# A whole network on one core: where group norms, keys, scores and experts get their turns and their PSUM places

## The chip, the cores and the metric

The kernel runs on one core of one Trainium2 chip. A core has five engines that this text names as the profile does: PE (matrix products; PEld is its loading of weights), DVE (vector), ACT (functions), POOL (GpSimd) and SP, which here only issues DMAs. Each runs its own list of instructions in order; they meet through semaphores. The metric is the device time of the one core, in microseconds, median of several runs: 15310.87 us before the change (15308.61 to 15326.58, three runs).

## The reference

The input x is 4 x 32 x 96 x 256, that is 4 batches of 3072 tokens with 256 channels, float32 throughout. Two layers are computed:

```python
x = x + mamba_d(mamba_t(group_norm(x)))          # two state space scans, along 96 and along 32
t = tokens(x)
t = t + attention(layer_norm(t))                 # additive attention, no matrix product of q and k:
#   h = tanh(q[:, :, None, :] + k[:, None, :, :] + bh);  e = h @ Wa;  softmax(e) @ inputs
t = t + experts(layer_norm(t), edges)            # gates from a graph, then 4 experts, 2 of them kept
#   per node: softmax over its incoming edges (1048576 random ones and one to itself), layer norm,
#   top 2 of 4 scores -> gate;  out = sum over e of gate[e] * (gelu(x @ W1[e] + b1[e]) @ W2[e] + b2[e])
```

group_norm has 32 groups of 8 channels, so each batch needs a mean and a variance of all its 3072 tokens before its first block can start. The additive attention needs a tanh for each triple of query, key and one of 32 units: 4 x 3072 x 3072 x 32 values, which are 3072 ACT instructions of 128 x 3072 here. An edge's gate input is a gathered table row, fetched by POOL with one indirect DMA for 128 edges.

## The kernel before

**Layer 0** (class Layer0, run) works in 64 blocks of 384 tokens: 8 of way t and 8 of way d for each of the 4 batches, with the first t block of the next batch drawn ahead. A block has 48 slots. The states of a block are scanned by DVE (L402) with decays from ACT (L385), inputs and outputs broadcast by DMA (bB, bC) and products on POOL (L409). While block n is scanned, front() prepares block n+1 in the same slots. The first 17 blocks ("lead") run alone, with more of the work on PE and ACT. group_norm (L99 to L132) stands before all of them: for each of 4 batches and 2 halves of the channels it loads the tokens in two halves (xs, two buffers), takes bn_stats on DVE, averages over the groups with two tiny matmuls, and takes the root on ACT.

**Attention** (units, L776 to L865) yields between its steps, and the main loop gives two steps of `steps()` to each iteration of units: half a slot of layer 0 each, as long as there is one, then sort and experts. An iteration issues one th (tanh, L815), scores two iterations later (L788, 16 PE records), and after 8 of them the unit's tail: maximum nb on DVE, exponential pr on ACT, transposes ptw, values pv. side is a list of small generators (keys of the next batch, the layer norm after attention); `beside()` advances the first by one step. keys(b) has 48 steps for a batch: 12 for statistics, then 12 groups of three (normalize, transpose through PE, project with PE and copy to krep and qsel). While a batch has no keys, an iteration issues no th:

```python
yield
late, self.later = self.later, []
for f in late:
    f()
yield
beside()
continue
```

The scores of a unit lie in `pe`, one place of two PSUM banks (pool "ate"). The first scores of a unit overwrite what pr of the unit before reads, so they are held back behind the iteration's second step (`held`).

**After layer 0** steps() gives an iteration to: the sort of the edges on DVE (class Edges, at EDGE_US of estimated work an iteration), the counting products on PE (L1233) and early experts (`early`, L1644 on), which draw on one budget of PE time: SLOT_US an iteration, less what the unit's own steps cost. Early experts put a first product into ph (pool "fp", two banks), copy it out with the bias on DVE (h), and their results (ko) go to DRAM (`kept`). Experts.bank chooses a pool by a turn that ph and po share.

**The tail** (tail, L1730 on) is a table of due times t. Three values of t are one expert unit (512 rows by one expert). Part m of 36 (12 columns of edges: scores, three times spread on DVE and place on PE) falls on t = G0 + PART * m // 2. `some` issues RATE gathers on POOL at each of its five calls a unit, each after a `pace` instruction that reads what ACT or DVE just wrote, so that POOL doesn't run ahead. When a quarter's parts are done, gates follow, and the kept results are loaded, gated and added.

Of the kernel before, what the change touches and what calls it, by code (L numbers as in the profile page):

```python
# [62 lines left out]
FIRST, RATE = 14, 2.75  # L63
G0, PART = 10, 6
KO_BUFS = 2
SLOT_US, PRODUCT_US = 1.2, 0.11
# [8 lines left out]
class Layer0:  # L75
# [8 lines left out]
    def __init__(self, ctx, tc, ident, a, x1):  # L84
# [12 lines left out]
        self.group_norm()  # L97

    def group_norm(self):  # L99

        nc, wk, ps, const = self.nc, self.wk, self.ps, self.const
        gavg = const.tile([P, P], F32, tag="gavg", name="gavg")
        nc.sync.dma_start(gavg, self.a["gavg"])
        eps = const.tile([P, 1], F32, tag="eps", name="eps")
        nc.vector.memset(eps, 1e-5)
        self.gm = const.tile([P, KC, B], F32, tag="gm", name="gm")
        self.gr = const.tile([P, KC, B], F32, tag="gr", name="gr")
        HB = TOK // 2
        NB = HB // 512
        for b in range(B):  # L110
            gm = self.gm[:, :, b]
            mv = wk.tile([P, KC, 2], F32, tag="gmv", name="gmv")
            gv = wk.tile([P, KC], F32, tag="gv", name="gv")
            for k in range(KC):
                stats = wk.tile([P, 2, NB, 6], F32, tag="gst", name="gst")
                for i in range(2):
                    xs = wk.tile([P, HB], F32, tag="dt", name="xs", bufs=2)
                    nc.sync.dma_start(xs, self.a["xT"][k * P:(k + 1) * P, b, i * HB:(i + 1) * HB])
                    for j in range(NB):
                        nc.vector.bn_stats(stats[:, i, j, :], xs[:, j * 512:(j + 1) * 512])  # L120
                nc.vector.bn_aggr(mv[:, k, :], stats.rearrange("p i n s -> p (i n s)"))
            pg = ps.tile([P, T], F32, tag="pp", name="pg")
            nc.tensor.matmul(pg[:, :KC], gavg, mv[:, :, 0], start=True, stop=True)
            nc.vector.tensor_copy(gm, pg[:, :KC])
# [4 lines left out]
            pg2 = ps.tile([P, T], F32, tag="pp", name="pg2")  # L129
            nc.tensor.matmul(pg2[:, :KC], gavg, gv, start=True, stop=True)  # L130
            nc.scalar.activation(self.gr[:, :, b], pg2[:, :KC], AF.Sqrt, bias=eps)
        nc.vector.reciprocal(self.gr, self.gr)  # L132
# [419 lines left out]
    def run(self):  # L552
# [34 lines left out]
        for n, blk in enumerate(blocks):  # L587
# [15 lines left out]
            ahead = self.front(then, blk["lead"]) if then and not breaks else {}  # L603
            for slot in range(48):
# [3 lines left out]
                for part in (left[1], jobs[1], ending, ahead):  # L608
# [31 lines left out]
class Attention:  # L640
# [4 lines left out]
    def __init__(self, ctx, tc, ident, a, x1, x2, xn2T, tab_s, tab_a):  # L645
# [7 lines left out]
        self.ps_e = pool("ate", PE_BUFS, space=PSUM)  # L653
# [122 lines left out]
    def units(self, side):  # L776
# [24 lines left out]
        while i < B * PER + LAG or todo or self.later:  # L801
            b, col = self.entry, self.col = divmod(i, PER)
            if b < B and "krep" not in self.state[b]:
# [3 lines left out]
                for f in late:  # L807
                    f()
                yield
# [15 lines left out]
            if behind and i >= LAG:  # L825
                n, k = divmod(i - LAG, NK)
                if k == 0:

                    pe = self.ps_e.tile([P, 2, JB], F32, tag="pe", name="pe")
# [743 lines left out]
class Experts:  # L1573
# [3 lines left out]
    def __init__(self, ctx, tc, x2, xn2T, gates, out, dram, beside=None):  # L1577
# [363 lines left out]
def whole(tc, a, dram, out):  # L1941
# [11 lines left out]
    with ExitStack() as ctx:  # L1953
        actx, lctx, ectx = ExitStack(), ExitStack(), ExitStack()
        with tc.manual_schedule(engines={E.PE, E.Activation, E.DVE, E.Pool}):
# [10 lines left out]
            def steps():  # L1966
# [7 lines left out]
                lctx.close()  # L1974
                keep = ctx.enter_context(tc.tile_pool(name="late", bufs=1))
# [134 lines left out]
```

## Time and profile before

The profiled execution took 15328.57 us (its span is 15326.8), 17.7 us above the median of the runs. Stages, from the busy time by stretch and the first and last th:

| stretch (us) | what runs | length |
|---|---|---|
| 0 to 62 | group norms of all batches | 62 |
| 62 to 2367 | first block's front, 17 lead blocks of 125 to 135 | 2305 |
| 2367 to 2566 | keys of batch 0, no th | 199 |
| 2566 to 11417 | th beside layer 0; from 5489 to 5574 no th (keys of batch 1) | 8851 |
| 11417 to 12450 | th beside the sort; 268 th | 1033 |
| 12450 to 14205 | th beside counts and early experts; 580 th | 1755 |
| 14205 to 15327 | rest of early experts, tail | 1122 |

Of the page, engines over the whole span, and slices in tenths:

```profile
PE 11744.9 (77%) x86496; PEld 5137.0 (34%) x86496; DVE 11006.6 (72%) x15895; ACT 12153.9 (79%) x9327; POOL 8997.6 (59%) x6935
...
DVE  7888888777777887777777877577778864321367
ACT  3443334999999979999999899999997889999221
POOL 4555556777777767767767677477750024400684
```

Shares over the whole span say little here, since each stage has another leader; the rows of slices show it: DVE in the first seven, ACT after, and no single one at the end. In a group's line "busy, mean ns | idle before" the last part names what ended the idle time of that engine before these instructions.

### The profile page before, as it was taken

To read this page: it belongs to the slowest core of one execution; us is meant where nothing else is said; L and a number is where in the kernel's file an instruction comes from. 1 tells how busy PE (TensorE), PEld (TensorE's weight loads), DVE (VectorE), ACT (ScalarE), POOL (GpSimd) and SP (SyncE) were. 2 spreads that over 40 slices of the span, in tenths; PEclk is the share of its full clock that TensorE was granted. 3 is DMA by queue.
4 is the path that set the end of the run, shared out by engine and by line. 5 is a ranking of instruction groups with operands and counts; after the bars stand their busy time and mean duration, and the time that the engine had idled before them with its cause. 6 is when DMAs were issued, how large, how long until landed. Compare 5 with 4: busy or idle time off the path is not lost. (4 is left out here: it accounts for less than half of the span.)

```text
span 15326.8 us, 225317 instructions
## 1 busy us (share of the span) xinstructions
PE 11744.9 (77%) x86496; PEld 5137.0 (34%) x86496; DVE 11006.6 (72%) x15895; ACT 12153.9 (79%) x9327; POOL 8997.6 (59%) x6935
## 2 busy tenths in 40 slices
PE   5666764777777767788887777888876778988997
PEld 2222332222222233333333333333332334433554
DVE  7888888777777887777777877577778864321367
ACT  3443334999999979999999899999997889999221
POOL 4555556777777767767767677477750024400684
PEclk8888887888888888989998889999988989999998
DMA  5666665445445444454454444355531000010234
GB/s 192 204 203 200 198 204 167 149 148 156 152 150 151 158 156 148 150 152 151 151 150 156 147 149 152 110 156 151 154 127 37 24 13 13 10 31 22 66 95 138
DMA packets 1209121, 2007.93 MB, mean 131 GB/s; under 512 B 412384, under 2 KB 655712, under 8 KB 1204960
## 3 DMA queue, kind: packets, MB, share of 16 engines
q1 hardware_dynamic: 1180384, 1988.07, 41.6%
q0 software_dynamic: 27648, 5.36, 0.8%
q8 instruction: 680, 11.14, 0.3%
q14 instruction: 409, 3.35, 0.1%
HBM read 1875.19 MB, written 117.83 MB: 130 GB/s over the span
## 5 line engine op out<-in xcount | busy, mean ns | idle before, releaser
L815 ACT ACTIVATE th<-krep,qsel 128x3072 f32<-128x3072 f32 x3072 | 8661.7, 2848 | 411.1 <-PE pe L788 392.0
L788 PE MATMUL pe<-th,wa_blk 128*32 128x384 f32 x49152 | 4999.3, 535 | 1196.7 <-ACT pr L884 957.3
L409 POOL TENSOR_TENSOR h<-h,bC 128x768 f32<-128x768 f32 x2048 | 3756.2, 1834 | 3000.4 <-DVE h L402 2634.4
L402 DVE TENSOR_TENSOR_SCAN h<-dA,dB 128x384 f32<-128x384 f32 x4096 | 3687.3, 942 | 1109.4 <-ACT dA L385 752.9
L788 PEld LDWEIGHTS pe<-th,wa_blk 128*32 128x32 f32 x49152 | 1448.0, 116 | 3775.6 <-issue 1992.1
L393 DVE TENSOR_TENSOR dB<-bB,dtu 128x768 f32<-128x768 f32 x2048 | 1942.3, 948 | 123.3 <-DMA bB<-bc 91.2
L385 ACT ACTIVATE dA<-dt,t_A 128x380 f32<-128x380 f32 x2048 | 1127.1, 571 | 887.6 <-DVE h L402 883.1
L385 ACT ACTIVATE dA<-dt,d_A 128x372 f32<-128x372 f32 x2048 | 1102.9, 562 | 601.3 <-DVE h L402 595.9
L428 PE MATMUL py<-h,ident 128*128 128x384 f32 x2176 | 1010.1, 597 | 679.6 <-POOL h L409 678.2
L416 POOL TENSOR_TENSOR h<-h 128x768 f32<-128x768 f32 x752 | 1423.0, 1892 | 53.6
L900 PE MATMUL pv<-xn,pT 128*32 128x257 f32 x18432 | 1116.1, 391 | 172.3 <-DVE pT L893 171.4
L959 POOL TENSOR_SCALAR sf<-sel,f 128x32 f32<-128x32 f32 x384 | 148.6, 410 | 1641.6 <-ACT f L955 1533.9
L893 DVE COPY pT<-ptw 128x512 f32<-128x512 f32 (+1 forms) x768 | 419.0, 546 | 703.7 <-PE ptw L891 703.0
L428 PEld LDWEIGHTS py<-h,ident 128*128 128x128 f32 x2176 | 445.4, 223 | 1247.6 <-POOL h L409 1015.2
L900 PEld LDWEIGHTS pv<-xn,pT 128*32 128x32 f32 x18432 | 583.5, 112 | 759.7 <-DVE pT L893 317.4
L417 POOL TENSOR_TENSOR h<-h 128x384 f32<-128x384 f32 x752 | 783.7, 1042 | 59.0
L418 POOL TENSOR_TENSOR y<-y,h 128x384 f32<-128x384 f32 x752 | 779.9, 1037 | 59.0
L1714 ACT ACTIVATE h<-ph,b 128x512 f32<-128x512 f32 x148 | 96.7, 685 | 662.9 <-POOL pace L1047 473.9
L1337 POOL DMA_INDIRECT gs<-tab_s,si x432 | 526.6, 1219 | 131.3 <-issue 98.8
L891 PE MATMUL ptw<-ident,pr 128*128 128x128 f32 x2304 | 484.7, 328 | 143.5 <-DVE pT L893 79.6
L902 DVE COPY pvs<-pv 128x257 f32<-128x257 f32 x384 | 160.2, 417 | 569.0 <-PE pv L900 568.8
L1052 POOL DMA_INDIRECT gd<-tab_a,di x432 | 467.2, 1082 | 140.6 <-issue 133.4
(302 smaller groups left out, 15311.0 us busy)
## 6 DMA issues: line engine op xcount, KB each, us to landing
bB<-bc SPq DMA_DIRECT2D x2048, 384.0 KB
bC<-bc SPq DMA_DIRECT2D x2048, 384.0 KB
all<-kept SPq DMA_DIRECT2D x24, 2048.0 KB
x<-x SPq DMA_DIRECT2D x144, 256.0 KB
kept<-ko SPq DMA_DIRECT2D x59, 512.0 KB
x<-x SPq DMA_DIRECT2D x192, 128.0 KB
xt<-xn2T SPq DMA_DIRECT2D x41, 512.0 KB
qsel<-xn2T SPq DMA_DIRECT2D x75, 256.0 KB
```

Source lines behind the costliest of these rows:

```text
L385: nc.scalar.activation(inner(dA[:, :T]), inner(blk["dt"][:, e, :]), AF.Exp, scale=blk["w"]["A"][:, e, i + s:i + s + 1])
L393: nc.vector.tensor_tensor(dB, blk["bB"].pop(j), z["dtu"].unsqueeze(1).to_broadcast([P, SB, T]), ALU.mult)
L402: nc.vector.tensor_tensor_scan(h[:, s, :], z.pop(("dA", e, i + s))[:, :T], z["dB"][:, s, :], 0.0, ALU.mult, ALU.add)
L409: nc.gpsimd.tensor_tensor(h, h, blk["bC"].pop(j), ALU.mult)
L416: nc.gpsimd.tensor_tensor(h0, h0, h1, ALU.add)
L417: nc.gpsimd.tensor_tensor(h0[:, 0, :], h0[:, 0, :], h0[:, 1, :], ALU.add)
L418: nc.gpsimd.tensor_tensor(y[e], y[e], h0[:, 0, :], ALU.add)
L428: nc.tensor.matmul(z["py"], self.ident, h[:, s, :], start=(i == 0), stop=(i == DS - 1))
L788: nc.tensor.matmul(pe[q * QU:(q + 1) * QU, j, :KQ // 2], self.wa[:, k, :], th[:, c0:c0 + KQ // 2], start=(k == 0), stop=(k == NK - 1))
L815: nc.scalar.activation(th, s["krep"], AF.Tanh, bias=s["qsel"][:, col:col + 1])
L900: nc.tensor.matmul(pv[q * QU:(q + 1) * QU, :C + 1], pT[:, i, q * QU:(q + 1) * QU], s["xn"][:, q * NK + i, :], start=(i == 0), stop=(i == N ...
L1337: nc.gpsimd.indirect_dma_start(out=gs[:, u, :], out_offset=None, in_=rows, in_offset=bass.IndirectOffsetOnAxis(ap=ed.si[:, q, c0 + u:c0 + ...
```

## The change

Group norms: group_norm(0) alone stands ahead, and the channels go through one tile of 3072 tokens (`wide("xs")`, the place that front's uab has too). Those of batches 1 to 3 are cut into pieces (norm_beside), put into slots of blocks 1 to 3 and 17 to 22. Keys: an iteration without keys calls beside() twice. Scores: once layer 0 has freed its PSUM, a second pool "ate2" of two banks is opened, and units alternates by `n // NK % 2`; with it nothing is held. Experts: pool "fp" has one bank instead of two, later three more; each tag counts its own turn; SLOT_US goes from 1.2 to 1.35. Tail: RATE from 2.75 to 3.2, PART from 6 to 5.

By the order of the two programs: iterations without th are 48, 19, 0 and 0 for the four batches before, and 24, 15, 10 and 0 after; early experts do 22 units before (18 with attention still running) and 29 after; the tail has 37 units before and 30 after. All other instructions are the same in number, but for the loads of weights and function tables that go with these and the paces of the tail.

```diff
@@ -60,10 +60,10 @@
 G1, K1 = 8, 4
 GP, GG = 12, 4
 EDGE_US = 2.4
-FIRST, RATE = 14, 2.75
-G0, PART = 10, 6
+FIRST, RATE = 14, 3.2
+G0, PART = 10, 5
 KO_BUFS = 2
-SLOT_US, PRODUCT_US = 1.2, 0.11
+SLOT_US, PRODUCT_US = 1.35, 0.11
 EU, EG = 32, 2
 TB = 512
 NQ, FC, NBLK_X = TB // P, FF // P, M // TB
@@ -94,42 +94,84 @@
         self.turn, self.beside = 0, None
         self.xt = [self.dram.tile([KC, P, NV, S], F32, tag="xt", name="xt", bufs=3)
                    for _ in range(B)]
-        self.group_norm()
...
+        self.norm_constants()
+        self.group_norm(0)
+        self.norms = [(b, k) for b in range(1, B) for k in range(KC + 1)]
+    def norm_constants(self):
+        nc, const = self.nc, self.const
+        self.gavg = const.tile([P, P], F32, tag="gavg", name="gavg")
+        nc.sync.dma_start(self.gavg, self.a["gavg"])
+        self.geps = const.tile([P, 1], F32, tag="eps", name="eps")
+        nc.vector.memset(self.geps, 1e-5)
         self.gm = const.tile([P, KC, B], F32, tag="gm", name="gm")
         self.gr = const.tile([P, KC, B], F32, tag="gr", name="gr")
...
+        self.gmv = const.tile([P, KC, 2], F32, tag="gmv", name="gmv")
+    def group_norm(self, b):
+        for k in range(KC):
+            for f in self.channel_norm(b, k):
+                f()
+        for f in self.factors(b):
+            f()
+    def channel_norm(self, b, k):
+        nc = self.nc
+        NB = TOK // 512
+        v = {}
+        def load():
+            v["x"] = self.wide("xs")
+            v["st"] = self.wk.tile([P, NB, 6], F32, tag="gst", name="gst")
+            for h in range(2):
+                cols = slice(h * TOK // 2, (h + 1) * TOK // 2)
+                nc.sync.dma_start(v["x"][:, cols], self.a["xT"][k * P:(k + 1) * P, b, cols])
+        def some(j):
+            nc.vector.bn_stats(v["st"][:, j, :], v["x"][:, j * 512:(j + 1) * 512])
+            if j == NB - 1:
+                nc.vector.bn_aggr(self.gmv[:, k, :], v["st"].rearrange("p n s -> p (n s)"))
+        return [load] + [lambda j=j: some(j) for j in range(NB)]
+    def factors(self, b):
+        nc, ps, mv, gm = self.nc, self.ps, self.gmv, self.gm[:, :, b]
+        v = {}
+        def mean():
+            v["pg"] = ps.tile([P, T], F32, tag="pp", name="pg")
+            nc.tensor.matmul(v["pg"][:, :KC], self.gavg, mv[:, :, 0], start=True, stop=True)
+        def variance():
+            nc.vector.tensor_copy(gm, v["pg"][:, :KC])
+            gv = v["gv"] = self.wk.tile([P, KC], F32, tag="gv", name="gv")
             nc.vector.tensor_tensor(gv, mv[:, :, 0], gm, ALU.subtract)
             nc.vector.tensor_tensor(gv, gv, gv, ALU.mult)
             nc.vector.tensor_tensor(gv, gv, mv[:, :, 1], ALU.add)
...
+        def mean2():
+            v["pg"] = ps.tile([P, T], F32, tag="pp", name="pg2")
+            nc.tensor.matmul(v["pg"][:, :KC], self.gavg, v["gv"], start=True, stop=True)
+        def root():
+            gr = self.gr[:, :, b]
+            nc.scalar.activation(gr, v["pg"][:, :KC], AF.Sqrt, bias=self.geps)
+            nc.vector.reciprocal(gr, gr)
+        return [mean, variance, mean2, root]
+    def norm_beside(self):
+        if not self.norms:
+            return {}
+        b, k = self.norms.pop(0)
+        if k == KC:
+            mean, variance, mean2, root = self.factors(b)
+            return {0: [mean], 1: [variance], 12: [mean2, root]}
+        return {slot: [f] for slot, f in zip((0, 10, 12, 14, 17, 20, 23), self.channel_norm(b, k))}
     def weights(self, way, keys, bufs=1):
@@ -601,11 +643,13 @@
             breaks = then and (then["way"], then["i"]) == ("d", 0) and then["b"] == blk["b"]
             jobs, later = self.back(blk, None if breaks else then)
             ahead = self.front(then, blk["lead"]) if then and not breaks else {}
+            norms = self.norm_beside() if n in (1, 2, 3) or n > 2 * NBLK else {}
             for slot in range(48):
                 for f in left[0].get(slot, []) + jobs[0].get(slot, []):
                     f()
                 yield None
-                for part in (left[1], jobs[1], ending, ahead):
+                for part in (left[1], jobs[1], ending, ahead, norms):
                     for f in part.get(slot, []):
                         f()
                 if slot == 12:
@@ -650,7 +694,7 @@
             tc.tile_pool(name=name, bufs=bufs, side="right", **k))
         const = self.const = pool("atc", 1)
         self.rows, self.th, self.wk = pool("atr", 2), pool("atb", TH_BUFS), pool("atw", 1)
-        self.ps_e = pool("ate", PE_BUFS, space=PSUM)
+        self.ps_e, self.ps_e2 = pool("ate", PE_BUFS, space=PSUM), None
         self.ps_v = pool("atv", PV_BUFS, space=PSUM)
         def load(name, shape, ap):
@@ -806,6 +850,7 @@
                 late, self.later = self.later, []
                 for f in late:
                     f()
+                beside()
                 yield
                 beside()
                 continue
@@ -825,8 +870,10 @@
             if behind and i >= LAG:
                 n, k = divmod(i - LAG, NK)
                 if k == 0:
-                    pe = self.ps_e.tile([P, 2, JB], F32, tag="pe", name="pe")
+                    places = self.ps_e2 if self.ps_e2 and n // NK % 2 else self.ps_e
+                    pe = places.tile([P, 2, JB], F32, tag="pe", name="pe")
+                if k == 0 and not self.ps_e2:
                     held = behind.pop(0)
                 else:
                     scores(pe, k, behind.pop(0))
@@ -1579,21 +1626,21 @@
         self.x2, self.xn2T, self.gates, self.out = x2, xn2T, gates, out
         pool = lambda name, bufs, **k: ctx.enter_context(tc.tile_pool(name=name, bufs=bufs, **k))
         self.xp, self.hp = pool("fx", 2), pool("fh", 2)
-        self.ps_h, self.ps_o = [pool("fp", 2, space=PSUM)], [pool("fo", 1, space=PSUM)]
+        self.ps_h, self.ps_o = [pool("fp", 1, space=PSUM)], [pool("fo", 1, space=PSUM)]
         self.kept, self.done = (beside.kept, beside.units()) if beside else ({}, [])
-        self.xts, self.turn = {}, 0
+        self.xts, self.turn = {}, {}
     def open(self, ctx, w):
         pool = lambda name, bufs, **k: ctx.enter_context(self.tc.tile_pool(name=name, bufs=bufs, **k))
         self.w = w
         self.io = pool("fi", 2)
-        self.ps_h.append(pool("fp2", 2, space=PSUM))
+        self.ps_h += [pool("fp2", 3, space=PSUM)] * 3
         self.ps_o.append(pool("fo2", 1, space=PSUM))
     def bank(self, pools, shape, tag):
-        self.turn += 1
-        return pools[self.turn % len(pools)].tile(shape, F32, tag=tag, name=tag)
+        self.turn[tag] = self.turn.get(tag, -1) + 1
+        return pools[self.turn[tag] % len(pools)].tile(shape, F32, tag=tag, name=tag)
     @staticmethod
     def weights(pool, nc, a):
@@ -1972,6 +2019,8 @@
                         side.append(att.keys(done))
                     yield
                 lctx.close()
+                att.ps_e2 = actx.enter_context(
+                    tc.tile_pool(name="ate2", bufs=1, side="right", space=PSUM))
                 keep = ctx.enter_context(tc.tile_pool(name="late", bufs=1))
                 late["gates"] = keep.tile([P, NH, NEXP], F32, tag="gates", name="gates")
                 ed = late["ed"] = Edges(ctx, tc, a, tab_a)
```

More of the change, by code (lines that the diff above doesn't have):

```diff
@@ L96, in __init__ @@
                    for _ in range(B)]
-        self.group_norm()
[L99 to L105, printed above, removed]
+        self.norm_constants()
+        self.group_norm(0)
+        self.norms = [(b, k) for b in range(1, B) for k in range(KC + 1)]
@@ L106, in group_norm @@
+    def norm_constants(self):
[4 more added lines that the diff above has]
+        nc.vector.memset(self.geps, 1e-5)
         self.gm = const.tile([P, KC, B], F32, tag="gm", name="gm")
         self.gr = const.tile([P, KC, B], F32, tag="gr", name="gr")
[L108 to L124, printed above, removed]
@@ L128, in group_norm @@
             nc.vector.tensor_tensor(gv, gv, mv[:, :, 1], ALU.add)
[L129 to L132, printed above, removed]
+        def mean2():
[14 more added lines that the diff above has]
+        return {slot: [f] for slot, f in zip((0, 10, 12, 14, 17, 20, 23), self.channel_norm(b, k))}
     def weights(self, way, keys, bufs=1):
```

## The prediction

> **What bounds the kernel now.** I read the page first (its 40 slices show four regimes), then the busy time by stretch, then for each stretch the groups of the engine that leads it, and last the order in time where two engines hand work to each other. The stretches (us, then busy time and count of PE, PEld, DVE, ACT, POOL, clock, DMA share, GB/s):
>
> ```profile
> 62.00:2367.00 2305.00, 1527.50 (x3368) 678.07 (x3368) 1942.68 (x2324) 928.38 (x1627) 1339.46 (x846) 0.86 0.63 199
> 2367.00:2566.00 199.00, 88.13 (x208) 50.38 (x208) 169.57 (x291) 49.22 (x81) 131.09 (x90) 0.63 0.56 175
> 2566.00:5489.00 2923.00, 2165.60 (x18892) 827.21 (x18892) 2291.92 (x3124) 2864.45 (x2163) 2188.10 (x1562) 0.88 0.49 151
> 5489.00:5574.00 85.00, 47.41 (x120) 29.41 (x124) 74.89 (x121) 20.87 (x35) 57.49 (x39) 0.66 0.49 159
> 5574.00:11417.00 5843.00, 4667.29 (x38392) 1989.59 (x38384) 4356.69 (x6209) 5547.26 (x4097) 4018.46 (x2888) 0.90 0.48 148
> 11417.00:12450.00 1033.00, 739.11 (x6634) 298.66 (x6634) 891.97 (x1404) 804.68 (x333) 24.00 (x33) 0.87 0.10 31
> 12450.00:14205.00 1755.00, 1554.76 (x15986) 710.81 (x15990) 563.06 (x1107) 1707.55 (x703) 479.66 (x720) 0.95 0.08 18
> 14283.00:15165.00 882.00, 814.75 (x2415) 470.35 (x2414) 523.49 (x927) 194.74 (x250) 742.03 (x735) 0.96 0.34 87
> ```
>
> Layer 0 alone is DVE's (84%). 2367 to 2566 is the wait for the first batch's keys and 5489 to 5574 that for the second's: DVE 85 to 88%, ACT nearly empty. Attention beside layer 0 is ACT's (95 to 98%). After layer 0 the sort is DVE's (86%) until 12450, then ACT leads again (97%), with PE close (89%). In the tail PE (92%) and POOL (84%) are both near full. POOL's groups from 14283 to 15165 settle who leads there, with ACT's gelu:
>
> ```profile
> L1337 POOL DMA_INDIRECT gs<-tab_s,si x422 | 517.1, 1225 | 106.6 <-issue 96.1 <-DVE y L1717 2.3 <-ACT h L1714 1.9
> L1052 POOL DMA_INDIRECT gd<-tab_a,di x104 | 116.8, 1123 | 27.9 <-issue 27.9
> L1047 POOL TENSOR_SCALAR pace<-h 128x32 f32<-128x32 f32 x141 | 68.7, 487 | 14.3 <-ACT h L1714 10.7
> L1714 ACT ACTIVATE h<-ph,b 128x512 f32<-128x512 f32 x136 | 88.7, 685 | 620.1 <-POOL pace L1047 473.9 <-PE ph L1632 145.8
> ```
>
> POOL's idle time there is issue gaps: it never waits for long, and gelu waits 474 us for POOL's pace. POOL holds the tail; PE is second.
>
> **The Trainium skill.** "ScalarE: Activation LUTs", What ACT_TABLE_LOAD costs: 1283 ns a load, and about 2.66 us with a drain. The trace agrees on the load (1283) and shows no drain: the gelu at 13018.81 starts as its load ends. I charge 1.28. "PSUM — Partial Sum Buffer", The four PSUM rules: eight banks of 512 fp32 columns; so a second place for scores (two banks) must take one from the experts. "SBUF — State Buffer", SBUF: two separate sides: DVE with two SBUF inputs and a GpSimd operation exclude each other; the gathers' mean of 1225 ns against about 1030 alone agrees.
>
> **Part A, group norms.** The factors of all four batches were there only here, and the first matmul ran at 62.5:
>
> ```profile
> 21.71 1.88 DVE L120 BATCH_NORM_STATS2 gst<-xs 128x6 f32<-128x512 f32 x3 [0.70 <-DMA xs<-in_xT]
> ...
> 60.23 0.20 DVE L132 RECIPROCAL gr<-gr 128x8 f32<-128x8 f32 x1 [0.97 <-ACT gr L131]
> ```
>
> Now one batch goes ahead, through one buffer: channel 0 done at 10.5, channel 1's load behind it (4.4 to the first half, 2.2 to the second, 1.9 + 0.3 of statistics) 19.4, factors 2.6: 22. SP's 10 loads before xin fit in the same time. Gain 38 us. Batch 1's norms (12 bn_stats of 0.63, two of 0.32 and the factors, 9 us of DVE, and 3 MB of loads on SP's queue ahead of the bB fetches) go into blocks 1 to 3, where DVE leads: +12 (0 to 25). Batches 2 and 3 add to ACT two Sqrts with two loads each (2 x 2.84 us): +6 (0 to 20); their DVE work lies under ACT. Sum: -20.
>
> **Part B, keys.** beside() is called twice in an iteration that has no keys. Counting the programs' order: waiting slots 48 and 19 become 24, 15 and 10 (a new one: batch 1 now ends before batch 2's keys). 18 waiting slots are replaced by attention. What a step costs DVE:
>
> ```profile
> 5530.65 0.68 DVE L718 COPY xTc<-pt 128x512 f32<-128x512 f32 x1
> ...
> 5535.20 0.92 DVE L752 COPY qsel<-pq 32x64 f32<-32x64 f32 x4 [1.85 <-PE pq L748]
> ```
>
> From the end of xTc to qsel PE needs 3.9 us; layer 0's DVE work stands between, the rest is waiting. With two steps a slot half as much stands between, so DVE waits about 2 to 3 us a group instead of 1.5. Durations of these rows set on the new order give, first wait: 127 us of DVE (185 before, less 61 for 24 layer-0 slots, plus 4 of norms) + 29 + 5 = 161, before 198. Second: 84 + 21 = 105, before 84.5. Third: 51 + 24 = 75, before none. Together +59 (10 to 80). Layer 0 lasts as many slots as before, so 18 more of them hold attention, at 3.9 us each: +70; 31 key steps fewer stand beside attention (blocks 33, 34, 49, 50 are some 1.2 us a step longer): -37; at the end 18 iterations go, at 1755/583 = 3.0 us with the idle of 0.1 kept: -53. Sum: +39: waits are shorter in slots, not in DVE time.
>
> **Part C, after layer 0.** One edit does less than it says. The place of the scores changes with n // NK % 2, n being the unit already: it changes every eighth unit. So seven of eight still wait for pr of the unit before, and the expert or count work that stood between (the held branch) now stands behind the first scores, with ptw behind that, all in PE's one order:
>
> ```profile
> 13713.07 0.96 DVE L877 TENSOR_REDUCE nb<-pe 128x1 f32<-128x768 f32 x1 [1.49 <-PE pe L788]
> 13715.72 0.88 ACT L884 ACTIVATE pr<-pe,nb 128x768 f32<-128x768 f32 x1
> ...
> 13716.65 1.50 PE L788 MATMUL pe<-th,wa_blk 128*32 128x384 f32 x16 [2.60 <-ACT pr L884]
> ```
>
> Here pr waits 1.7 us after nb, for ACT: that is PE's lead. Moving 0.7 to 1.1 us of work behind the wait, and 0.8 more of expert work a unit (6.5 more units over 104), takes most of it. ACT needs 8 x 2.745 + 0.88 = 22.8 us a unit; PE about 15.9 + 5.9, plus 2.0 of nb and pr latency, less 0.9 hidden in it, 22.9. I take 0.2 us a unit, 22 us (0 to 85). ph's one bank hardly tells: between two f a score group stands in all but 12 places before attention ends. More expert units before attention ends: two in the sort, DVE 4 x 0.75 + 2 x 0.68 each, 9, with 3 for PE; the others 4.5 x 1.9 + 2 pairs of loads x 2.57 = 13 on ACT. Sum: +47 (15 to 110). The rest of early after attention: +5.
>
> **Part D, tail.** 30 units instead of 37: PE saves 7 x 13.8 us (16 x 0.429 + 32 x 0.216, start to start) = 97, and po, whose two calls a unit fell on the same pool by the shared count, alternates (28 us of waits). But POOL keeps all its 540 gathers at about 1.42 with their gaps; only 33 paces go, 33 x 0.54 = 18 us. Its last gather comes 18 earlier, 5 later from the start, some 10 later from denser DVE work. Behind the last gather stood 162 us; now units end before it, and part 35, the gates and the last blocks' loads (about 10 us a block, two buffers) follow: 115 to 125. So -3 - 42 = -45 (-120 to -20). RATE and PART can't hurry POOL: parts ask for 16 gathers in 2.5 slots.
>
> **Sum:** -20 + 39 + 47 + 5 - 45 = +26. The profiled execution is 15328.6 us, 17.7 above the median of 15310.9; against the median 15337 us. What can be told from no change is 0.2%, 31 us; +26 stands just inside, so the sides are close.
>
> **Rivals.** (1) PE becomes the bound after layer 0: each of 104 units costs 0.8 us instead of 0.2, +61: 15398. For: PE's need of 22.9 already stands on ACT's 22.8, bursts of expert work now come straight behind the wait. Against: gelu pairs of about 6.4 us on ACT let PE catch up. It decides when th's idle behind pe from 11417 to 14205 passes 250 us (170 now). (2) The other side, faster: PE and not POOL sets the tail, so that all of 97 + 24 us less 11 comes back, -110 instead of -45: 15272. For: PE 92% busy. Against: 474 us of gelu behind pace. It decides if a gather with its gap falls under 1.3 us. (3) Key steps cost DVE no more when doubled (other work fills the wait), so the waits stay at 282: 15278. Against: one psum place, copy, product and copy in a row.
>
> **Chances.** The forecast 0.45, (1) 0.30, (2) 0.15, (3) 0.10. With some 35 us around the forecast it is slower by more than 0.2% in 0.44 of its cases and faster in 0.05; (1) is nearly always slower; (2) and (3) are faster in a little over half. Faster 0.17, within 0.2% 0.35, slower 0.48. The range takes in the gains of (2) and (3) and the upper bound of part C: 15260 to 15430.
>
> **What would show it.** A: first px matmul at 24 to 26 us; the first block at 67 instead of 105. B: three waits of about 160, 105 and 75 us without th, qsel waiting 2 to 3 us for pq. C: pe of the first scores waiting longer for pr than the 154 us of 12450 to 14205, th's idle at 190 to 230 over both stretches. D: from the first pace to the last gs near 880 us still, with some 120 us behind it instead of 162, and gelu still waiting for pace. The prediction is wrong if the waits together stay under 300 us, if pe no longer waits for pr (then the places do alternate), or if the tail loses over 80 us.

## The result and the profile after

The changed kernel takes 15396.07 us (median of five runs, 15390.30 to 15409.80), the kernel before 15314.58 in the same comparison: ratio 1.0052, 95% interval 1.0041 to 1.0063. It is slower, by some 81 us, where +26 was forecast. The profiled executions differ by the same 81 us in their spans (15326.8 and 15407.8), so they can be compared stage by stage.

The stretches of the kernel after (start and length, then busy time and count of PE, PEld, DVE, ACT, POOL, the clock, DMA share and GB/s). They are cut at its waits for keys, at the last step of layer 0 (11468), at 12500, near the end of the sort, and at the first and last gather of the tail. Not all of the cuts are those of the kernel before: there the last step of layer 0 is at 11378.7, not at the 11417 of the table of stages, and its line of the tail starts with the first pace. The table below uses the same marks for both.

```profile
23.50:2336.00 2312.50, 1525.13 (x3372) 676.17 (x3372) 1951.29 (x2340) 931.29 (x1630) 1337.87 (x846) 0.85 0.63 200
2336.00:2479.50 143.50, 67.98 (x176) 41.00 (x176) 107.54 (x228) 23.62 (x41) 63.29 (x44) 0.65 0.51 152
2479.50:5429.50 2950.00, 2193.21 (x18868) 832.21 (x18868) 2317.93 (x3131) 2878.46 (x2170) 2181.26 (x1561) 0.86 0.49 151
5429.50:5535.00 105.50, 56.07 (x131) 34.99 (x132) 78.97 (x133) 18.36 (x29) 50.08 (x35) 0.58 0.39 118
5535.00:8623.00 3088.00, 2474.07 (x20262) 1049.38 (x20260) 2376.66 (x3384) 2950.75 (x2209) 2188.48 (x1568) 0.90 0.49 152
8623.00:8692.00 69.00, 37.77 (x109) 24.07 (x110) 42.51 (x79) 8.76 (x16) 29.06 (x20) 0.65 0.39 125
8692.00:11468.00 2776.00, 2221.60 (x18210) 937.07 (x18213) 2000.50 (x2823) 2627.42 (x1927) 1867.92 (x1346) 0.89 0.47 144
11468.00:12500.00 1032.00, 755.71 (x6702) 315.99 (x6694) 850.49 (x1260) 806.03 (x332) 31.06 (x38) 0.90 0.12 36
12500.00:14292.00 1792.00, 1592.39 (x16100) 743.51 (x16104) 634.86 (x1301) 1711.98 (x709) 478.11 (x720) 0.96 0.09 21
14335.50:15247.60 912.10, 805.43 (x2323) 453.29 (x2321) 536.61 (x937) 191.49 (x242) 742.46 (x717) 0.94 0.32 83
15247.60:15407.80 160.20, 33.82 (x64) 14.51 (x64) 121.81 (x259) 3.65 (x6) 0.38 (x1) 0.60 0.53 185
```

The three short stretches with ACT nearly empty are the waits for keys: 143.5, 105.5 and 69.0 us, where before there were two, of 198 and 82 between the last th and the next. Behind each stands a long one in which ACT is at 95 to 98%. The last two are the tail's gathers (912 us) and what stands behind the last of them (160 us). From the marks in both traces ("keys asked for" is the first statistics instruction of batch 0's keys, "end of attention" the end of the last th):

| from to | before us | after us | difference | forecast for it |
|---|---|---|---|---|
| start to batch 0's keys asked for | 2367.6 | 2335.9 | -32 | -26 (A: -38 + 12) |
| keys asked for to the end of attention | 11836.9 | 11956.3 | +119 | +92 (A 6, B 39, C 47) |
| of it, last step of layer 0 to the end of attention (859 th before, 841 after) | 2825.8 | 2824.2 | -2 | -6 (C 47, of B -53) |
| end of attention to the end | 1122.3 | 1115.6 | -7 | -40 (D -45, left over 5) |

Two stages miss, by 27 and by 33 us, and most of the 27 lies before layer 0 ends. The tail's groups on POOL and then ACT's gelu with what it waited for, between the first and the last gather:

```profile
L1384 POOL DMA_INDIRECT gs<-tab_s,si x432 | 505.2, 1169 | 139.8 <-issue 107.0 <-DMA tab_a<-db 27.1 <-DVE y L1764 1.6
L1099 POOL DMA_INDIRECT gd<-tab_a,di x108 | 129.4, 1198 | 31.3 <-issue 28.2 <-ACT v L1322 1.2 <-ACT h L1761 0.9
L1094 POOL TENSOR_SCALAR pace<-h 128x32 f32<-128x32 f32 x119 | 84.8, 713 | 12.1 <-ACT h L1761 9.2
L1094 POOL TENSOR_SCALAR pace<-ko 128x32 f32<-128x32 f32 x57 | 22.7, 398 | 1.3
```

```profile
L1761 ACT ACTIVATE h<-ph,b 128x512 f32<-128x512 f32 x120 | 76.6, 686 | 464.0 <-POOL pace L1094 398.4 <-PE ph L1679 65.3
```

POOL still has no long wait and gelu still waits 398 us for pace: POOL holds the tail as before. There are 33 paces fewer, but one "pace from h" takes 713 ns instead of 487, and all paces together take 84.8 + 22.7 = 107.5 us, against 108.5 in the kernel before over the same stretch.

### The profile page after: what moved, and what is told of

The parts are those of the page before. It is cut to its first block, busy times and chain, and to the rows that moved or that the text cites. A ratio compares the mean times of both kernels' runs of the same rounds, so it can differ in the third digit from the quotient of the medians.

```text
span 15407.8 us, 225389 instructions
## 1 busy us (share of the span) xinstructions
PE 11798.3 (77%) x86496; PEld 5143.4 (33%) x86496; DVE 11042.9 (72%) x15926; ACT 12164.1 (79%) x9317; POOL 8971.5 (58%) x6902
## 5 line engine op out<-in xcount | busy, mean ns | idle before, releaser
L947 PE MATMUL pv<-xn,pT 128*32 128x257 f32 x18432 | 1126.4, 394 | 108.9 <-DVE pT L940 108.5
L924 DVE TENSOR_REDUCE nb<-pe 128x1 f32<-128x768 f32 x384 | 362.6, 944 | 351.0 <-PE pe L832 350.9
```

Of the source, the lines that this page charges most:

```text
L947: nc.tensor.matmul(pv[q * QU:(q + 1) * QU, :C + 1], pT[:, i, q * QU:(q + 1) * QU], s["xn"][:, q * NK + i, :], start=(i == 0), stop=(i == N ...
```

## The experiments

Each ratio is to the kernel before, measured beside it on the same chip; "us" below is the ratio's interval times the time before. The first four share one group of runs, the next four another, the last four a third (medians of the kernel before: 15320.10, 15318.16, 15329.74). The edits are shown by their main lines. Six kernels (`c_alone`, `c_slot12`, `slot135`, `c_n2`, `after_noD`, `best`) also have `next(gathers, None)` for `next(gathers)` in the tail; it only lets the list of gathers end quietly, and all 14 kernels issue 540 gathers there.

**The parts alone.** First, the norms only (`a_alone`):

```diff
 # before, with
-        self.group_norm()
+        self.norm_constants()
+        self.group_norm(0)
+        self.norms = [(b, k) for b in range(1, B) for k in range(KC + 1)]
...
+            norms = self.norm_beside() if n in (1, 2, 3) or n > 2 * NBLK else {}
```

> The kernel before with the group norms of the change alone. My sum: -38 us in front, +12 in the lead blocks, +6 beside attention: about -20 us. The rival, from the trace of the changed kernel, where the keys of batch 0 are asked for 32 us earlier: if the norms beside attention cost nothing, -32 us; if they are what made that kernel's first batch of attention 23 us longer, -10 us or less.

Ratio 0.9986 (0.9979 to 0.9993), -32 to -11 us, median 15298.18. First px at 23.5, keys asked for at 2339.2 instead of 2367.6. Batch 0's attention 2929 us instead of 2927. The part does what its sum said. From the first px to the first keys it takes 2287 to 2305 us in the traces of the nine kernels whose lead blocks are those of before, and 2309 to 2316 in the five that have the norms there: a single pair of traces is good to some 18 us, but the means are 12 apart, the +12 of the sum.

The keys only (`b_alone`):

```diff
                 for f in late:
                     f()
+                beside()
                 yield
                 beside()
```

> The kernel before with the second beside() alone. My sum: waits +59 us, 18 more slots of attention beside layer 0 +70, key steps no longer beside attention -37, 18 iterations fewer at the end -53: about +39 us, with waits near 161, 105 and 75 us. The rival: key steps are hidden, the waits stay at 282 us in sum, and the kernel is 20 us faster or the same.

Ratio 1.0040 (1.0025 to 1.0054), +38 to +83, median 15383.86: more than expected, and the rival, a gain, is out. The three waits in its trace:

```profile
2350.00:2493.40 143.40, 66.72 (x176) 40.93 (x176) 104.92 (x222) 23.44 (x40) 63.05 (x44) 0.64 0.49 153
5435.40:5541.20 105.80, 56.45 (x131) 35.03 (x132) 78.88 (x132) 18.27 (x29) 50.19 (x35) 0.58 0.37 117
8635.00:8704.20 69.20, 37.91 (x109) 24.14 (x110) 42.62 (x80) 8.72 (x17) 29.04 (x20) 0.63 0.39 126
```

318 us against 280: the first wait falls by 54, the second rises by 24, and a third of 69 us is new. From the keys asked for to the end of attention it takes 11914.0 us, +77; so only half of it is waits. The other half, by the th between the waits:

| th of | before us | b_alone us | difference | forecast for it |
|---|---|---|---|---|
| batch 0 (768 th) | 2927 | 2942 | +15 | -37 for this row and the next (31 key steps fewer) |
| batch 1 (768) | 3139 | 3094 | -46 | |
| batch 2, to the last step of layer 0 (677 before, 695 in b_alone) | 2663 | 2771 | +108 | +70 (18 slots more) |
| the rest (859 before, 841 in b_alone) | 2826 | 2788 | -38 | -53 (18 iterations fewer) |

The third row is not only 18 slots more. Late in layer 0 the same 704 scans beside 566 th (565 in `b_alone`) make a stretch of 2216 us in the kernel before and of 2255 in `b_alone`. Here it is in both, with what th waited for:

```profile
8986.00:11202.00 2216.00, 1805.92 (x14948) 775.41 (x14949) 1625.88 (x2306) 2137.61 (x1564) 1503.66 (x1085) 0.92 0.48 145
L815 ACT ACTIVATE th<-krep,qsel 128x3072 f32<-128x3072 f32 x566 | 1602.8, 2848 | 60.1 <-PE pe L788 59.4
```

```profile
9042.00:11297.00 2255.00, 1845.49 (x14950) 789.96 (x14946) 1614.37 (x2300) 2137.01 (x1561) 1499.21 (x1079) 0.90 0.47 143
L816 ACT ACTIVATE th<-krep,qsel 128x3072 f32<-128x3072 f32 x565 | 1599.2, 2846 | 94.8 <-PE pe L788 94.5
```

ACT does the same work and waits 35 us longer for the scores. PE takes 1845 us instead of 1806 for as many multiplications, at a granted clock of 0.90 instead of 0.92. Whether the slower multiplications are the cause of the wait, or both come from the new order, no run settles.

The second place, the banks' turn and the larger share (`c_alone`):

```diff
+                    places = self.ps_e2 if self.ps_e2 and n // NK % 2 else self.ps_e
...
+        self.ps_h += [pool("fp2", 3, space=PSUM)] * 3
...
-SLOT_US, PRODUCT_US = 1.2, 0.11
+SLOT_US, PRODUCT_US = 1.35, 0.11
```

> The kernel before with the PSUM places, the bank turns and SLOT_US of 1.35 alone. Theory (POOL holds the tail): +47 us before attention ends, and of the seven units that the tail loses only the paces come back, 18 us: +20 to +35 us. The rival (PE holds the tail): the tail is 90 to 120 us shorter, so the whole is 40 to 70 us faster.

Ratio 1.0017 (1.0010 to 1.0023), +15 to +35, median 15345.40: as expected. The end of attention comes 2862.8 us after the last step of layer 0 instead of 2825.8 (+37), the tail takes 1105.8 instead of 1122.3 (-16).

The tail's rate and part alone (`d_alone`):

```diff
-FIRST, RATE = 14, 2.75
-G0, PART = 10, 6
+FIRST, RATE = 14, 3.2
+G0, PART = 10, 5
```

> The kernel before with RATE 3.2 and PART 5 alone. Theory (POOL holds the tail): the 540 gathers and 209 paces take as long as before, 0 us within 15; gelu goes on waiting for pace. The rival: denser parts let the last gather come sooner and the time after it shrinks, -40 us.

Ratio 1.0003 (0.9995 to 1.0012), -8 to +18, median 15325.98: no difference that can be told. But inside the tail two things moved against each other: gathers 904.8 us instead of 918.6, and 180.8 behind the last gather instead of 161.5. The expectation kept 209 paces; the trace has 176, since with more gathers a call fewer calls do. So the 33 paces that the changed kernel saves come with RATE alone too; with the 30 units and the old rate 29 are saved. The medians of the four differ from before by -22, +64, +25 and +6, together +73 of the 81.

**Which piece of C costs.** The two places and the banks without the larger share (`c_slot12`), and the share without them (`slot135`):

```diff
 # c_slot12: c_alone, with
-SLOT_US, PRODUCT_US = 1.35, 0.11
+SLOT_US, PRODUCT_US = 1.2, 0.11
 # slot135: before, with
-SLOT_US, PRODUCT_US = 1.2, 0.11
+SLOT_US, PRODUCT_US = 1.35, 0.11
```

> Part C without its larger share: the two places for the scores (changing every eighth unit), no held work, the new order of banks; experts' share, keys and norms as in the kernel before. All of C alone gave +25: +37 between the last step of layer 0 and the end of attention, -16 in the tail. Theory 1, what costs is the larger share (more expert units beside attention, each with gelus and table loads on ACT): this kernel is at 0 to +8, and last layer-0 step to the end of attention stays near 2826 us. Theory 2, what costs is the new place of the expert work behind the first scores: +25 to +40, with 2850 to 2865 us there. The tail keeps its 37 units and 1120 us in both.

> The counterpart: the larger share alone, one place for the scores, the held work and the shared turn of banks as before. Theory 1 (the share costs): last layer-0 step to the end of attention 2855 to 2865 instead of 2826, tail 16 shorter, the whole +15 to +25. Theory 2 (the order behind the scores costs): 2830, and with the shorter tail the whole is at -10 to -16.

`c_slot12`: ratio 1.0017 (1.0010 to 1.0024), +15 to +37. `slot135`: 0.9988 (0.9982 to 0.9995), -28 to -8. So theory 2: the share gains, the places lose. In detail each theory had a part: from layer 0 to the end of attention the places cost 23 us (2848.5) and the share 16 (2842.1), but the share takes 28 out of the tail (1094.2). "Places" means the two places with the new banks and without held work; no run took these apart.

Then the place that changes every unit (`c_n2`):

```diff
-                    places = self.ps_e2 if self.ps_e2 and n // NK % 2 else self.ps_e
+                    places = self.ps_e2 if self.ps_e2 and n % 2 else self.ps_e
```

> All of part C with one change: the place of the scores alternates with n % 2, every unit, instead of n // NK % 2, every eighth. If PE's wait for pr was worth something after layer 0, pe's idle behind pr falls from about 900 us in the whole run to that of the time beside layer 0, PE gets a lead over ACT, th's idle behind pe falls by some 100 us after layer 0, and the whole comes to -30 to -60 against before. If PE's wait is hidden by ACT, which has no more than the same work, the whole stays at +15 to +30 as part C alone.

Ratio 0.9984 (0.9977 to 0.9991), -35 to -14, median 15294.91 where `c_alone` had 15345.40. The groups of the scores on PE and of th on ACT from the last step of layer 0 to the end of attention (busy time and mean ns, then the idle time before them and what ended it), before, `c_slot12` and `c_n2` in this order:

```profile
L788 PE MATMUL pe<-th,wa_blk 128*32 128x384 f32 x13768 | 1361.9, 523 | 331.0 <-ACT pr L884 312.8 <-ACT th L815 17.8
...
L815 ACT ACTIVATE th<-krep,qsel 128x3072 f32<-128x3072 f32 x859 | 2394.0, 2848 | 178.6 <-PE pe L788 173.9 <-POOL pace L1047 2.0 <-PE pm L938 1.1
```

```profile
L788 PE MATMUL pe<-th,wa_blk 128*32 128x384 f32 x13768 | 1363.5, 523 | 296.5 <-ACT pr L886 273.7 <-ACT th L815 22.4
...
L815 ACT ACTIVATE th<-krep,qsel 128x3072 f32<-128x3072 f32 x859 | 2396.4, 2848 | 200.7 <-PE pe L788 196.1 <-POOL pace L1049 1.5 <-PE pm L940 1.1
```

```profile
L788 PE MATMUL pe<-th,wa_blk 128*32 128x384 f32 x13760 | 1323.4, 509 | 74.2 <-ACT th L815 51.6 <-ACT pr L886 21.8
...
L815 ACT ACTIVATE th<-krep,qsel 128x3072 f32<-128x3072 f32 x859 | 2387.2, 2848 | 154.6 <-PE pe L788 153.2 <-POOL pace L1049 0.5
```

With the turn after eight units th loses 22 us more behind pe, which is as much as the places cost in this stage. `c_n2` has the larger share too, so its counterpart with one place is `slot135`:

```profile
L788 PE MATMUL pe<-th,wa_blk 128*32 128x384 f32 x13760 | 1335.9, 514 | 265.2 <-ACT pr L884 240.7 <-ACT th L815 24.2
L815 ACT ACTIVATE th<-krep,qsel 128x3072 f32<-128x3072 f32 x859 | 2392.7, 2848 | 168.2 <-PE pe L788 166.6 <-POOL pace L1047 1.0
```

With a turn each unit, PE's wait for pr is gone (241 to 22 us), but of those 219 us only 13 reach th: PE's wait was mostly hidden. The stage is 23 us shorter than in `slot135`, the whole 7 us in the medians, with intervals that overlap. So a turn each unit is worth some 50 us against one after eight units, but two places are worth little against one; most of the gain over the kernel before is the share's. The expected 100 us less of th's idle and -30 to -60 overall were too much.

The same edit in the full changed kernel (`after_n2`):

```diff
 # the changed kernel, with
-                    places = self.ps_e2 if self.ps_e2 and n // NK % 2 else self.ps_e
+                    places = self.ps_e2 if self.ps_e2 and n % 2 else self.ps_e
```

> The changed kernel with the place of the scores changing every unit (n % 2) and nothing else. If the every-eighth turn is the fault also in company of the key steps: -40 to -55 against the changed kernel, 15340 to 15355, pe's waits for pr after layer 0 nearly gone. If the key steps leave no room for it: as the changed kernel, 15390 to 15400.

Median 15353.36, ratio to before 1.0015 (1.0008 to 1.0022), against the changed kernel's 1.0052: some 57 us back. The last step of layer 0 to the end of attention takes 2762.0 us instead of 2824.2. The every-eighth turn costs as much in company.

**Whether the first wait's gain can be kept.** The second key step for batch 0 only (`b_first`):

```diff
+                if b == 0:
+                    beside()
                 yield
                 beside()
```

> The kernel before with the second key step for the first batch only. Waiting slots by the programs' order: 24, 29 and 7 (before 48, 19, 0; with both steps for all batches 24, 15, 10). Theory 1, ACT leads from the first th to the end of attention, so only its idle time counts: waits of 143, 29 x 4.45 = 129 and 7 x 4.5 = 31, together 303 us against 280, and 7 more slots' work of layer 0 on ACT beside attention (some 0.9 us each), +6: +25 to +35 in all, and what the first wait loses comes back in the second, since layer 0 delivers the rows no sooner. Theory 2, the prediction's sum of slots: waits +23, 7 slots more beside layer 0 at 3.9 = +27, 7 fewer at the end at 3.0 = -21, 17 key steps fewer beside attention at 1.2 = -20: +9. Theory 3, the first wait's gain of 54 us stays: -40 to -54.

Ratio 1.0009 (1.0001 to 1.0017), +2 to +26, median 15336.32. Theory 3 is out: the first wait's 54 us came back in the second and third wait. They fell as worked out:

```profile
2354.00:2497.60 143.60, 67.20 (x176) 41.33 (x176) 104.28 (x222) 23.44 (x40) 62.95 (x43) 0.65 0.50 152
5437.80:5567.40 129.60, 65.94 (x176) 39.36 (x180) 115.47 (x170) 30.71 (x51) 86.69 (x60) 0.66 0.47 154
8668.70:8698.70 30.00, 17.63 (x73) 10.12 (x75) 27.91 (x48) 7.08 (x13) 19.21 (x13) 0.72 0.60 195
```

303 us. The whole lies at the lower edge of theory 1 or below it, and near theory 2, so the run does not separate these two by itself. The groups of th over the whole span, in before, `b_alone` and `b_first`:

```profile
L815 ACT ACTIVATE th<-krep,qsel 128x3072 f32<-128x3072 f32 x3072 | 8661.7, 2848 | 411.1 <-PE pe L788 392.0 <-DVE krep L755 11.4 <-POOL pace L1047 2.0
```

```profile
L816 ACT ACTIVATE th<-krep,qsel 128x3072 f32<-128x3072 f32 x3072 | 8664.2, 2847 | 438.2 <-PE pe L788 405.8 <-DVE krep L755 24.5 <-POOL pace L1048 3.7
```

```profile
L817 ACT ACTIVATE th<-krep,qsel 128x3072 f32<-128x3072 f32 x3072 | 8664.7, 2848 | 387.9 <-PE pe L788 365.3 <-DVE krep L755 16.1 <-POOL pace L1049 2.2
```

th itself is the same work in all three. Its idle time behind pe is +14 in one and -27 in the other. Counted on ACT, from the keys asked for to the end of attention: `b_alone` has 38 us of longer waits, 20 of layer 0's own ACT work that no longer runs inside the waits (ACT is busy there for 23.4 + 18.3 + 8.7 = 50.4 us, before 49.2 + 20.9 = 70.1), and 14 behind pe: 72 of the 77. `b_first` has 23, 9 and -27: 5 of 14 (11851.2 less 11836.9), so some 5 to 9 us stay uncounted.

**The tail.** Without the pace (`no_pace`):

```diff
-            if credit[0] >= 1:
-                ed.behind(t)
```

> The kernel before, with the pace instruction of the tail left out (a GpSimd copy whose only use is to put the gathers behind the work of a slot). If GpSimd sets the tail: its 106 or so paces of 0.49 us and their gaps go, 0.54 each, and the last gather comes 55 to 60 us earlier, the whole at -45 to -60. If PE sets it: gathers run ahead to the limit of their buffers, the units keep 26.5 us each, and the whole stays within 15 us of before.

Ratio 0.9953 (0.9936 to 0.9969), -98 to -48, median 15245.81. POOL, not PE, set the gathers' stretch. The expectation counted the paces from h only; with those from ko there are 209, 108.5 us. The edit also lets gathers run ahead of the units, so the gain is not the paces' price alone. The stretch from the first to the last gather and what stands behind it:

```profile
14231.50:15074.60 843.10, 818.82 (x2504) 478.72 (x2503) 534.21 (x941) 210.77 (x263) 671.23 (x541) 0.99 0.39 97
15074.60:15240.30 165.70, 72.98 (x216) 40.80 (x214) 131.56 (x268) 12.36 (x17) 1.80 (x2) 0.75 0.51 183
```

843 us instead of 919, with PE now at 97%: the two limits lie close together.

The changed kernel with the old rate and part (`after_noD`):

```diff
 # the changed kernel, with
-FIRST, RATE = 14, 3.2
-G0, PART = 10, 5
+FIRST, RATE = 14, 2.75
+G0, PART = 10, 6
```

> The changed kernel with rate and part of the tail as before (2.75 and 6) and nothing else. Theory 1: the denser parts ask for gathers sooner than GpSimd brings them, PE's scores wait in order, and the expert units behind them are stretched to 31 us; with the old values they run at 26.5 us and end some 150 us before the last gather, and what stands behind that falls from 160 to about 130: the tail at 1100 to 1106 us instead of 1116, the whole 10 to 20 under the changed kernel. Theory 2: the number of units alone decides, and the tail stays at 1112 to 1118 us.

Ratio 1.0046 (1.0030 to 1.0061), median 15395.05: the interval covers the changed kernel's 1.0052, so no gain is shown. The same two stretches:

```profile
14320.50:15263.20 942.70, 792.47 (x2314) 449.26 (x2312) 546.81 (x962) 179.68 (x230) 745.50 (x722) 0.92 0.33 83
15263.20:15395.50 132.30, 34.54 (x74) 14.60 (x72) 112.32 (x235) 3.65 (x6) 0.05 (x1) 0.66 0.55 199
```

Behind the last gather stand 132 us instead of 160, as theory 1 said, but the gathers take 31 longer, so the tail is 1118.6 us. Its units' gelus start mostly 23 to 29 us apart once under way, those of the changed kernel mostly 28 to 35, and its last gelu ends 156 us before the last gather, not 33. Part of the 31 us is not the kernel's: two units' gelus among the first five start 52 us apart, and so they do in all four kernels of this group (52 to 55; in the other groups no more than 31, and `after_n2`'s gathers take 928 us where the changed kernel's take 912). It is looked at in the last section.

The edits that gained, together (`best`):

```diff
 # the changed kernel, with
-                beside()
...
+                    places = self.ps_e2 if self.ps_e2 and n % 2 else self.ps_e
...
+FIRST, RATE = 14, 2.75
+G0, PART = 10, 6
...
-            if credit[0] >= 1:
-                ed.behind(t)
```

> What the runs speak for, together: the norms (-22), two places for the scores that alternate every unit with the larger share and the new banks (-22), no pace in the tail (-71), keys, rate and part as before. If all add: -115, 15203 us. The share's gain in the tail was mostly the paces of its 33 fewer calls (18 us), which are gone without pace: then -97, 15221 us. If the tail without pace is PE's, the fewer units give more than that: under 15200.

Ratio 0.9953 (0.9939 to 0.9966), -94 to -52, median 15246.30. Faster than both kernels, but no faster than `no_pace`. Its attention ends at 14166.8, 38 us before that of the kernel before; the tail gives back what the sum lacks: 1077.7 us against 1051.0 in `no_pace`. Its gathers:

```profile
L1383 POOL DMA_INDIRECT gs<-tab_s,si x432 | 534.6, 1237 | 207.4 <-issue 123.1 <-DVE v L1322 50.7 <-DMA tab_a<-db 27.0
```

Without pace POOL runs ahead until its buffers are full and then waits 51 us for DVE's v. Tighter parts for this kernel were not tried.

## Why the prediction was right in direction and small in size

**A, -20.** Right: -22 alone. First px was put at 24 to 26, it is at 23.5, and the first scan follows at 67.7 in the kernel after (67 forecast); of those 39 us 28 are left when the keys are asked for (+12 for blocks 1 to 3 was forecast, 11 measured in this pair, 12 between the means above).

**B, +39.** Right in sign, +64 measured, +77 in the trace from the keys asked for to the end of attention. Term by term:

- Waits, "+59": +39. They were forecast at 161, 105 and 75 and are 143, 106 and 69. That qsel waits 2 to 3 us for pq came true (2.2, 2.1 and 3.5 on average). The first wait is off by 18 us, and 14 of these are a slip: the "185 before" adds up DVE's rows with their overlaps, while the line of 2367 to 2566 shows DVE busy for 169.57.
- Key steps, "-37": -31, the first two rows of the table of `b_alone`, in which all 31 lie. That it was these steps is not shown: in `b_first` only 7 steps fewer lie beside batch 1, and its row falls by 38 all the same.
- The end, "-53": -38.
- "18 more of them hold attention, at 3.9 us each: +70": +108. This is the step that failed. A slot more costs 6.0 us here, and 6.2 in `b_first` (7 slots, 43 us).

What stands in place of the last is th's idle time behind pe, 37 us more of it in that row of `b_alone`, nearly all of the 38 that were missed (in `b_first` 9 of 16). Up to the last step of layer 0, batch 2 has 68 to 76 us of it in the nine kernels with the old order of key steps and 105 to 111 in the four with the second step for all batches; for batch 1 it is 120 to 124 and 77 to 85. So it goes with the order and is not scatter, and the forecast, which priced a slot by its old mean, had no term for it. Why the order moves it is open.

**C, +47 in attention.** Right in mechanism: +37. "I take 0.2 us a unit, 22 us" for PE's lead was 23, and more expert units 16 instead of 25. The forecast read from the diff that the place changes every eighth unit; `c_n2` and `after_n2` show that this is what costs, and `slot135` that a place which alternates every unit gains little over one. A stretch of the timeline of the kernel after shows the new order:

```profile
13574.80 0.95 DVE L924 TENSOR_REDUCE nb<-pe 128x1 f32<-128x768 f32 x1
...
13575.79 0.90 ACT L931 ACTIVATE pr<-pe,nb 128x768 f32<-128x768 f32 x1 [2.58 <-DVE nb L924]
...
13576.74 1.83 PE L832 MATMUL pe<-th,wa_blk 128*32 128x384 f32 x16 [2.62 <-ACT pr L931]
...
13578.51 0.89 PE L1280 MATMUL pc<-hot_keep 128*128 128x96 bf16 x8
...
13579.22 1.05 PE L938 MATMUL ptw<-ident,pr 128*128 128x128 f32 x4
```

Here ACT has stood for 2.58 us until nb came, so pr follows it at once; the first scores wait 2.62 us for pr, and the count work (pc) that could have filled that stands behind them. One mark was wrong: pe waits less for pr than before, 181 us against 313 over the whole stage, not more. A reason may be that PE gets to that place later, so that less of the wait is left to it. The mark that counted was th's idle time behind pe, forecast at 190 to 230 and 190 in the kernel after. Rival 1's point, 250 us, was not reached; that its 15398 us lie near the measured time is chance.

**D, -45.** The larger miss: -7. The mechanism held, as gelu went on waiting for pace and POOL had no long wait; two terms failed.

The first is "Behind the last gather stood 162 us; now units end before it ... 115 to 125": 160 were measured. With 30 units and the old rate and part it was 134 us in `slot135`, 133 in `c_alone` and 132 in `after_noD`, two thirds of the gain. The new rate and part take it back, and in `d_alone` they make 181 out of 162. The forecast dismissed them with "RATE and PART can't hurry POOL". The gathers did end sooner with them, but the units were stretched until they ended with the gathers. The likely way is that the parts ask sooner for gathers and the units stand behind them on PE and behind pace on ACT; the runs show the stretch and not which wait makes it. Together the two effects cancel: the tail takes 1115.6 us with the new values and 1118.6 without.

The second is "only 33 paces go, 33 x 0.54 = 18 us". In the changed kernel those that stay cost more, 107.5 us against 108.5. In `slot135` all paces took 77.6 us, 31 less, but the gathers cost 1225 ns on average instead of 1198 and POOL stood idle for 17 us more, so the stretch was 920 us as before. With the old rate and part the whole tail gained 28 us in `slot135`, 22 in `c_n2`, 16 in `c_alone` and 4 in `after_noD`, never the 45.

So of the 55 us between forecast and result the tail makes 33, the keys with what lies beside attention 27, less 6 for the lead, which is within the scatter of the lead blocks. None of the three signs of being wrong showed: the waits are 318 us, pe still waits for pr, the tail loses 7. With +26 inside the 31 us that can't be told from no change, the right sign was not much of a test.

## What to carry to other kernels

Find the engine that leads a stage and book a change there in that engine's busy and idle time. Slots priced at one old mean gave -20 for all that lay outside the waits, where +39 came, while the leading engine's wait moved with the order, up beside one batch and down beside another. In this tail, which POOL's own instructions held, taking a fifth of the units out gave 4 to 28 us, and a schedule that asked for gathers sooner only moved time from the gathers to what stands behind them. Read an index of a rotation to the end: the second place that changes every eighth turn had the cost of the new order without the overlap. And time busy, not the sum of rows that overlap, is what a stretch holds.

## What the runs showed of the hardware

The same small instruction on GpSimd had one price alone and many beside DVE. A pace from h, 128 x 32 values, took 487 ns on average in the tail of the kernel before, 713 in the changed one, 408 in `slot135`, and one from ko 586, 398 and 478. Put beside DVE's instructions in the trace, the averages come apart. In the kernel before, each of the 96 paces that ran while DVE ran nothing took 0.29 to 0.33 us; the 112 that overlapped a DVE instruction with two input tensors (TENSOR_TENSOR, its scan, SCALAR_TENSOR_TENSOR) took 0.70 on average and up to 2.3. Of the 540 gathers, the 207 without DVE took 0.94 to 1.03 us, the 328 beside such an instruction 1.34 on average and up to 2.96. The changed kernel shows the same prices alone, 0.31 to 0.32 for a pace and at most 1.03 for a gather. So a sum with 0.54 us a pace could be off by all of its gain.

In three of the four kernels of the third group PE had a stretch at the start of the tail in which its instructions came late without a wait that the profile shows; here in `best` (start, length, then the idle time before it; 9 multiplications took 4.03 us just ahead of it):

```profile
14290.63 0.52 PE L1686 MATMUL po<-w,h 128*128 128x256 f32 x1 [1.01 <-issue]
14293.43 0.58 PE L1686 MATMUL po<-w,h 128*128 128x256 f32 x1 [2.29 <-issue]
14296.23 0.59 PE L1686 MATMUL po<-w,h 128*128 128x256 f32 x1 [2.21 <-issue]
```

From 14288 to 14323 there are 14 such gaps of 25.8 us together; `after_n2` and `after_noD` have 12 and 9 of over 0.6 us, 15.6 and 10.1 us together. `b_first`, the fourth, has none on PE, but ACT stands there for 13.6 us in the same way. No kernel of the other groups shows such gaps on PE, and the kernel before is 10 to 15 us longer in this group than in the others, so it may be in all of the group's kernels. The cause stays open.
